# Two graph layers on one core: an earlier read of one bank, the setup work in single pieces, and another order in the last group

## The chip, the core and the metric

The kernel runs on one core of a Trainium2 chip. The metric is the device time of one execution in microseconds (us). The engines are named as in the profile: PE (TensorE, matmuls), PEld (PE's weight loads), DVE (VectorE), ACT (ScalarE), POOL (GpSimd), SP (SyncE, which issues most DMAs here).

## What is computed

The input x is 64 batches of 256 tokens with 512 features, in float32. Cut to what matters, with `h` of the shape of x:

```python
def _layernorm(x, eps=1e-5):
    m, v = mean(x, -1), var(x, -1)
    return (x - m) / sqrt(v + eps)

# layer 0
h = maximum(_layernorm(x), 0)
y = einsum('nm,bmd->bnd', adj, h)
x = x + einsum('bnd,do->bno', y, weight) + bias
# layer 1
h = maximum(_layernorm(x), 0)
q, k, v = h @ Wq + bq, h @ Wk + bk, h @ Wv + bv          # 8 heads of 64
scores = einsum('bqhd,bkhd->bhqk', q, k) / sqrt(64)
scores = scores + (1 - adj) * -1e9
attn = softmax(scores)
x = x + (attn applied to v) @ Wo + bo
```

## The kernel before

**Tiles and groups.** A group is two batches (GB = 2), so there are 32 groups (NG). All of layer 0 runs first, group by group; it leaves each group's residual and its normalized hidden state in DRAM. Then layer 1 runs, group by group.

**Projections.** Each 512x512 projection of a group is done by `project` (L441) in the manner of Strassen and Winograd, on blocks of 256: seven products instead of eight. A product (`product`, L433) is eight matmuls of 128x128 on 256 columns. Three sums of weight blocks (s1, s2, s4, and s3 in place of a block) come from `weight_sums` (L400), once per weight, in four operations (L409 or L411); four sums of data blocks (t1 to t4) come from `Halves.sums` (L427, L431), once per group and projection. The products go into four PSUM banks, called a, b, c and d. The order is: A11·B11 into a, read as u1; A12·B21 into b, finished with u1; S2·T2 added into a, read as u2; S1·T1 into c; S3·T3 added into a, read as u3; then c is finished with u3, and a is released; A22·T4 into d, finished with u3; S4·B22 added into c, finished with u2. In q and k a read makes a partial u on ACT with the bias (L629, two operations of 128x256), and a finish is DVE's add (L485) of a bank and a partial. In v a read is one ACT copy (L646). In layer 0 (prefix w) and in the output projection (prefix o) no partial is made: read and finish both add the bank on DVE straight into a quarter of the residual x, which `RESIDUAL` (L488) names. There a "read" with index 4 adds bank a once more. Partials come from the pool tag "u", which has three buffers.

**Layer 0.** `layer0` (L519): 32 matmuls multiply the adjacency with the group's h (L531, tiles py), ACT copies the result to yT (L541), POOL makes t1 to t4 (tile t_y, L431), and `project` follows. DVE takes statistics of the finished quarters (L582, L587), and ACT makes the next hidden state. The normalization of the input of group g + 2 (`ready`, L491: DVE statistics L42, POOL scales L53 and L54, ACT L506, POOL's bias add L510) is placed between these steps.

**Layer 1.** Per group: `attend` (L713: sums of exponents with `pden` L720, weighted values `pav` L727, reciprocals on DVE L737, division L744, then the sums t_o of the output projection), `score` (L675: products sc L686, scaled and masked on DVE L691, less a bound `top` per query on POOL L697 or, for half of the last group, on DVE L701), exponents on ACT (L704) and sums over keys on POOL (L711, tiles as). Score and attend work on half of the heads at a time (qd 0 and 1). Around them stand `queries_keys` (L617) and `values` (L638) of the next group and `post` (L654), the output projection of the group before. L810 adds the output bias to the residual on POOL.

**What sets the order.** The schedule is by hand. Each engine runs its instructions in the order in which the program issues them. `after(delay, ...)` (L259) puts a piece of work on a list, and `tick()` (L263) issues what is due; `run` (L751) steps a generator, with one tick for each step, so a layer-0 group is eleven ticks: four of the adjacency product and seven of `project`. PSUM banks come from a first-in first-out list (L246, L252). Setup work is hung on layer-0 groups by the list `side` (L757 to L764): the loads of the layer-1 weights, their sums on POOL (for q, k, v, o in groups 4, 6, 8, 10, in ticks 6 to 9), the product of v's bias with Wo (`out_bias`, tile pbo, L387, group 9), and the mask and the bound top from the adjacency (`masks`, L333, groups 12 to 14). In the end, a small product (pf, L833) and a copy (flag, L834) of a test on the statistics of the softmax sums (bad, worst, L828, L829) stand within the last group's output projection, in which S1·T1 comes second. The test decides if a general path is run; in all of these runs it isn't.

Of the kernel before, what the change touches and what calls it, by code (L numbers as in the profile page):

```python
# [198 lines left out]
def kernel(  # L199
# [52 lines left out]
    def give(t):  # L252
        free_banks.append(bank_of.pop(id(t))[0])
# [80 lines left out]
    def masks():  # L334
        adj_sb = tmp.tile([P, NT, N], F32, tag="u", name="adj_sb")
        nc.sync.dma_start(adj_sb, adj.rearrange("(t p) m -> p t m", p=P))
        yield
        pm = bank([P, NT, N], "pm")
        for k in range(NT):
            for t in range(NT):  # L340
                nc.tensor.transpose(pm[:, k, t * P:(t + 1) * P], adj_sb[:, t, k * P:(k + 1) * P], ident)
        nc.vector.tensor_scalar(maskT, pm, -1.0, 1.0, op0=ALU.mult, op1=ALU.add)
        give(pm)
        nc.vector.tensor_scalar(maskT, maskT, MASKED, None, op0=ALU.mult)
        nc.vector.tensor_scalar(adj_sb, adj_sb, -1.0, 1.0, op0=ALU.mult, op1=ALU.add)
        nc.vector.tensor_scalar(adj_sb, adj_sb, MASKED, None, op0=ALU.mult)
        rowmax = small.tile([P, NT], F32, tag="rowmax", name="rowmax", bufs=1)
        nc.vector.tensor_reduce(rowmax, adj_sb, AX.X, ALU.max)
        spread = tmp.tile([P, NT, P], F32, tag="u", name="spread")
        nc.vector.tensor_copy(spread, rowmax[:, :, None].to_broadcast([P, NT, P]))  # L350
        yield
        pt = bank([P, N], "pt")
        for t in range(NT):
            nc.tensor.transpose(pt[:, t * P:(t + 1) * P], spread[:, t, :], ident)
        nc.vector.tensor_copy(top, pt)
        give(pt)
# [23 lines left out]
    def out_bias():  # L380

        wo_sb, bo_r, bv_c = L1["o"]
        bvb = tmp.tile([P, DC, P], F32, tag="u", name="bvb")
        nc.vector.tensor_copy(bvb, bv_c[:, :, None].to_broadcast([P, DC, P]))
        ps = bank([P, D], "pbo")
        for d in range(DC):
            nc.tensor.matmul(ps, bvb[:, d, :], wo_sb[:, d, :], start=(d == 0), stop=(d == DC - 1))  # L387
        nc.vector.tensor_tensor(bo_r, ps, bo_r, op=ALU.add)
        give(ps)
# [7 lines left out]

    W = {}

    def weight_sums(eng, w, n, spread=False):  # L400

        def part(i, j):
            return w[:, 2 * j:2 * j + 2, i * HF:(i + 1) * HF]
        s = {m: const.tile([P, 2, HF], F32, name=f"w{n}_{m}") for m in ("s1", "s2", "s4")}
        ops = ((s["s1"], part(1, 0), part(1, 1), ALU.add), (s["s2"], s["s1"], part(0, 0), ALU.subtract),
               (part(1, 0), part(0, 0), part(1, 0), ALU.subtract), (s["s4"], part(0, 1), s["s2"], ALU.subtract))
        for i, (o, p, q, op) in enumerate(ops):
            if spread:
                after(6 + i, lambda o, p, q, op: eng.tensor_tensor(o, p, q, op=op), o, p, q, op)  # L409
            else:  # L410
                eng.tensor_tensor(o, p, q, op=op)  # L411
        W[n] = dict(s, a11=part(0, 0), a12=part(0, 1), a22=part(1, 1), s3=part(1, 0))

    class Halves:
# [25 lines left out]

    def project(s, halves, by_token, name, read, finish, first_half_first=False):  # L441

        def new(n):
            return bank([P, 2, N], f"{name}{n}")
        pa = new("a")
        product(pa, s, "a11", halves, "b11", by_token, stop=False)
        u1 = read(pa, 1)
        yield
        if first_half_first:
            pc = new("c")  # L450
            product(pc, s, "s1", halves, "t1", by_token, stop=False)
            yield
        pb = new("b")
        product(pb, s, "a12", halves, "b21", by_token)
        finish(pb, u1, 0, 0)
        give(pb)
        yield
        product(pa, s, "s2", halves, "t2", by_token, start=False, stop=False)
        u2 = read(pa, 2)
        yield  # L460
        if not first_half_first:
            pc = new("c")
            product(pc, s, "s1", halves, "t1", by_token, stop=False)
            yield
        product(pa, s, "s3", halves, "t3", by_token, start=False)
        u3 = read(pa, 3)
        finish(pc, u3, 1, 1)
        read(pa, 4)
        give(pa)
        yield  # L470
        pd = new("d")
        product(pd, s, "a22", halves, "t4", by_token)
        finish(pd, u3, 1, 0)
        give(pd)
        yield
        product(pc, s, "s4", halves, "b22", by_token, start=False)
        finish(pc, u2, 0, 1)
        give(pc)
        yield
# [5 lines left out]
        nc.vector.tensor_tensor(o, ps, u, op=ALU.add)  # L485


    RESIDUAL = {1: (0, 0), 2: (0, 1), 3: (1, 1), 4: (1, 0)}  # L488


    def ready(g, moments_at, scales_at, relus_at, biases_at, batches=1):  # L491
# [125 lines left out]
    def queries_keys(g):  # L617

        for n, store in (("q", Q), ("k", K)):
            store[g] = {}  # L620
            bias = L1[n][1]

            def read(ps, m):
                if m == 4:
                    return
                u = partial(f"{n}_{g}", m)
                for c in range(2):
                    f = 2 * (m == 3) + c
                    nc.scalar.activation(u[:, c, :], ps[:, c, :], AF.Identity, bias=bias[:, f:f + 1])  # L629
                return u  # L630

            def finish(ps, u, i, k):
                o = store[g][i, k] = act.tile([P, 2, N], F32, tag=f"{n}{i}{k}", name=f"{n}_{g}_{i}{k}")
                add(o, ps, u)

            yield from project(W[n], HH[g], False, f"{n}_{g}", read, finish)

    def values(g):  # L638
        v = act.tile([P, HQ, GB, NT, HF], F32, tag="yT0", name=f"v_{g}")
        V[g] = {(i, k): v[:, i, k] for i in range(HQ) for k in range(GB)}  # L640

        def read(ps, m):
            if m == 4:
                return
            u = partial(f"v_{g}", m)
            nc.scalar.copy(u, ps)  # L646
            return u

        def finish(ps, u, i, k):
            add(V[g][i, k], ps, u)  # L650

        yield from project(W["v"], HH.pop(g), True, f"v_{g}", read, finish)

    def post(g):  # L654

        xt = X.pop(g)
        halves = HO.pop(g)
        done = []

        def read(ps, n):  # L660
            o = quarter(xt, *RESIDUAL[n])
            add(o, ps, o)

        def finish(ps, u, i, k):
            o = quarter(xt, i, k)
            add(o, ps, o)
            done.append(k)
            if done.count(k) == 2:
                nc.sync.dma_start(out[g * GB + k].rearrange("(t p) d -> p t d", p=P), xt[:, k * NT:(k + 1) * NT, :])

        yield from project(W["o"], halves, True, f"o_{g}", read, finish, first_half_first=g == NG - 1)
# [3 lines left out]
    def score(g, qd, sum_delay):  # L675


        tail = []
        pair = [act.tile([P, GB, 2 * NT, N], F32, tag="h", name=f"a_{g}_{qd}_{c}", bufs=2) for c in range(2)]
        for c in range(2):  # L680
            for b in range(GB):
# [8 lines left out]
                for j in range(2):  # L690
                    nc.vector.scalar_tensor_tensor(a[:, j * NT:(j + 1) * NT, :].rearrange("p k n -> p (k n)"),  # L691
                                                   ps[j], SCALE, maskT_f, op0=ALU.mult, op1=ALU.add)
                    give(ps[j])
                if g == NG - 1 and c == 1:
                    tail.append(a)
                else:
                    nc.gpsimd.tensor_tensor(a, a, top_b, op=ALU.subtract)  # L697
                after(3 + 2 * c + b, exponent, a)
                after(sum_delay + 2 * c + b, key_sum, g, qd, c, b)
        for a in tail:  # L700
            nc.vector.tensor_tensor(a, a, top_b, op=ALU.subtract)  # L701

    def exponent(a):
        nc.scalar.activation(a, a, AF.Exp)  # L704
# [8 lines left out]
    def attend(g, qd):  # L713
# [28 lines left out]
        def divide():  # L742
            for f in range(2):
                nc.vector.tensor_tensor(OT[g][:, 2 * qd + f, :], po[f], rden, op=ALU.mult)  # L744
                give(po[f])
            nc.scalar.activation(den, rden, AF.Identity, accum_out=stats[:, 1, i:i + 1])  # L746
            HO[g].sums(nc.gpsimd if g < NG - 1 else nc.vector, ("t1",) if qd == 0 else ("t2", "t3", "t4"))

        after(1 if g < NG - 1 or qd else 8, divide)

# [4 lines left out]


    side = [[] for _ in range(NG)]  # L757
    mask_steps = masks()
    for i, n in enumerate("qkvo"):
        side[2 + 2 * i].append((load_layer1, n))  # L760
        side[4 + 2 * i].append((lambda n: weight_sums(nc.gpsimd, L1[n][0], n, spread=True), n))
    side[9].append((out_bias,))
    for i in range(3):
        side[12 + i].append((lambda: next(mask_steps, None),))  # L764

    ready(0, (0, 0, 2, 2), (0, 2), (1, 1, 3, 3), (5, 5, 6, 6), batches=2)
    load(1)
    tick()
    turn_adjacency()
    tick()  # L770
    weight_sums(nc.vector, w0_sb, "0")
    load(2)
    tick()
    tick()
# [27 lines left out]
    for g in range(NG):  # L802
# [13 lines left out]
        if g + 1 < NG:  # L816
# [3 lines left out]
            if g + 2 < NG:  # L820
                hidden_sums(g + 2, 2, 3, 4, 5)
                run(post(g))
    while later:
        tick()

    bad = tmp.tile([P, 2 * NG * HQ], F32, tag="u", name="bad")
    worst = small.tile([P, 1], F32, tag="worst", name="worst", bufs=1)
    nc.vector.tensor_scalar(bad, stats.rearrange("p s i -> p (s i)"), BOUND, None, op0=ALU.is_gt)  # L828
    nc.vector.tensor_reduce(worst, bad, AX.X, ALU.max)  # L829
    last = post(NG - 1)  # L830
    run(last, 4)
    pf = bank([1, 1], "pf")
    nc.tensor.matmul(pf, worst, ones[:, 0:1], start=True, stop=True)  # L833
    nc.vector.tensor_copy(flag, pf)  # L834
# [36 lines left out]
```

## Time and profile before

| what | value |
|---|---|
| three runs | 2760.43, 2757.74, 2760.40 us, median 2760.4 |
| the profiled execution's own time | 2759.62 us |
| its span | 2757.9 us |
| granted PE clock, mean | 0.997 |
| PE busy | 2719.9 us, 99% of the span |
| POOL, DVE, ACT busy | 1817.7, 1554.9, 803.6 us |
| 32 layer-0 adjacency products, each | 6.91 us on the chain |
| layer-1 group | 65.40 us from one to the next |
| clock at 0.50 | 194.03 to 200.86, 702.62 to 706.03, 2723.31 to 2726.72 us |

The page's first part gives the busy time of each engine over the whole span. The waits give, for PE, what released it after it had been idle. The chain follows the work that ended last back to the start: a row is a start, a duration and what ran then, or "issue" where the profile shows nothing that was waited for. The timeline gives each instruction's start and duration; in brackets stands how long its engine had been idle before, and who released it. A busy time counts the whole time of an instruction in flight, so neighbouring products overlap by some 0.16 us in the timeline, and the chain's durations are those that add up.

### The profile page before, as it was taken

The numbers are of one execution on the slowest core, as the hardware profiler recorded it, in microseconds if no ns is written. First come the engines' busy times: TensorE is split into PE (matmuls) and PEld (weight loads), VectorE is DVE, ScalarE is ACT, GpSimd is POOL, SyncE is SP. The second block draws the span as 40 slices with busy tenths as digits, with TensorE's granted clock in tenths as the row PEclk, the third lists the DMA queues.
The fourth block names the chain that finished last, engine by engine and source line by source line (L and its number), as shares of the span: only waits on it lengthen the run. The fifth ranks groups of instructions, "written<-read, shape, count | busy, mean of one in ns | idle before, by whom it ended". The sixth has DMA issues, their size and how long they took to land.

```text
span 2757.9 us, 43345 instructions
## 1 busy us (share of the span) xinstructions
PE 2719.9 (99%) x17172; PEld 2242.2 (81%) x17172; DVE 1554.9 (56%) x2783; ACT 803.6 (29%) x1377; POOL 1817.7 (66%) x1424
## 2 busy tenths in 40 slices
PE   8989999999999999999999999999999999999997
PEld 7878888888788888888888888888888888888886
DVE  7877877775455444444555444445555544444456
ACT  3333344342222222222222222222222222222221
POOL 6777676674666666666666666666666666666664
PEclk9999999999999999999999999999999999999999
DMA  7666666663122111111111111111222211111110
GB/s 180 181 170 160 163 170 160 170 160 93 36 61 56 47 47 47 47 46 47 47 47 46 47 47 46 47 47 47 62 62 58 51 47 47 47 46 47 47 47 32
DMA packets 280478, 210.50 MB, mean 76 GB/s; under 512 B 145872, under 2 KB 211920, under 8 KB 280272
## 3 DMA queue, kind: packets, MB, share of 16 engines
q1 hardware_dynamic: 279808, 207.15, 29.0%
q8 instruction: 138, 2.26, 0.3%
q10 hardware_dynamic: 464, 0.52, 0.1%
q14 instruction: 68, 0.56, 0.1%
HBM read 106.96 MB, written 100.66 MB: 75 GB/s over the span
## 4 chain that ended last, share of the span: by engine, by line
PE 95%; DVE 2%; POOL 1%; DMA 1%; issue 1%; ACT 0%; SPq 0%; ACTq 0%; DVEq 0%; POOLq 0%
PE sc L686 8%; PE pav L727 8%; PE py L531 7%; PE pden L720 2%; DVE x L485 1%; DVE a L691 0%; POOL a L697 0%; DMA w_sb<-in_L_gnn_weight_dram 0%; DVE st L582 0%; PE pbo L387 0%; PE o_31a L438 0%; ACT h L561 0%; PE w_1a L438 0%; PE q_29a L438 0%; PE q_27a L438 0%
## 5 line engine op out<-in xcount | busy, mean ns | idle before, releaser
L697 POOL TENSOR_TENSOR a<-a,top 128x1024 f32<-128x1024 f32 x252 | 587.2, 2361 | 711.1 <-DVE a L691 711.1
L691 DVE SCALAR_TENSOR_TENSOR a<-sc,maskT 128x512 f32<-128x512 f32 x512 | 311.9, 680 | 26.8 <-PE sc L686 26.8
L711 POOL TENSOR_TENSOR as<-a 128x512 f32<-128x512 f32 x256 | 319.5, 1288 | 0.0
L704 ACT ACTIVATE a<-a 128x1024 f32<-128x1024 f32 x256 | 264.0, 1057 | 21.5 <-POOL a L697 20.3
L737 DVE RECIPROCAL den<-den 128x128 f32<-128x128 f32 x256 | 216.8, 909 | 71.5 <-ACT den L734 71.4
L686 PE MATMUL sc<-q,k 64*128 64x256 f32 x2048 | 238.4, 383 | 0.0
L727 PE MATMUL pav<-a,v 128*32 128x256 f32 x4096 | 233.2, 379 | 0.0
L686 PEld LDWEIGHTS sc<-q,k 64*128 64x128 f32 x2048 | 194.2, 187 | 44.7 <-issue 26.3
L531 PE MATMUL py<-adjT,h 128*128 128x256 f32 x1024 | 228.7, 382 | 0.9 <-DVE adjT L325 0.9
L531 PEld LDWEIGHTS py<-adjT,h 128*128 128x128 f32 x1024 | 196.1, 192 | 28.5 <-ACT h L506 1.2
L734 ACT ACTIVATE den<-pden 128x512 f32<-128x512 f32 x64 | 38.2, 597 | 594.5 <-issue 459.9
L727 PEld LDWEIGHTS pav<-a,v 128*32 128x32 f32 x4096 | 133.4, 110 | 87.7
L561 ACT ACTIVATE h<-x,nb,rs 128x512 f32<-128x512 f32 x128 | 97.2, 806 | 351.8 <-POOL nb L54 351.7
L510 POOL TENSOR_TENSOR x<-x,b_r 128x512 f32<-128x512 f32 x128 | 160.4, 1284 | 1.0 <-ACT h L506 0.9
L810 POOL TENSOR_TENSOR x<-x,bo_r 128x512 f32<-128x512 f32 x128 | 158.5, 1279 | 0.0
L53 POOL TENSOR_TENSOR rs<-rs,mhalf 128x2 f32<-128x2 f32 (+1 forms) x97 | 78.0, 804 | 117.3 <-DVE nb L52 117.3
L431 POOL TENSOR_TENSOR t_y<-yT,t_y 128x256 f32<-128x256 f32 (+1 forms) x96 | 87.3, 910 | 56.5 <-ACT yT L541 53.9
L746 ACT ACTIVATE den<-den 128x512 f32<-128x512 f32 x64 | 40.4, 632 | 221.4 <-DVE den L737 221.4
L582 DVE BATCH_NORM_STATS2 st<-x 128x6 f32<-128x256 f32 x256 | 96.4, 418 | 4.4
L506 ACT ACTIVATE h<-x,nb,rs 128x512 f32<-128x512 f32 x128 | 93.9, 806 | 10.3 <-POOL nb L54 10.3
L431 POOL TENSOR_TENSOR t_y<-yT 128x256 f32<-128x256 f32 (+1 forms) x96 | 88.0, 917 | 12.3 <-ACT yT L541 9.3
L42 DVE BATCH_NORM_STATS2 st<-x 128x6 f32<-128x512 f32 x128 | 84.9, 663 | 6.5 <-DMA x<-in_x_dram 6.5
(2952 smaller groups left out, 5499.8 us busy)
## 6 DMA issues: line engine op xcount, KB each, us to landing
x<-in_x_dram SPq DMA_DIRECT2D x256, 128.0 KB, 3.5
residual<-x SPq DMA_DIRECT2D x256, 128.0 KB, 2.3
hidden<-r SPq DMA_DIRECT2D x128, 256.0 KB, 4.7
h1T<-hidden SPq DMA_DIRECT2D x64, 512.0 KB, 9.7
x<-residual SPq DMA_DIRECT2D x32, 1024.0 KB, 6.7
out_dram<-x SPq DMA_DIRECT2D x64, 512.0 KB, 3.3
w_sb<-in_L_gnn_weight_dram SPq DMA_DIRECT2D x1, 1024.0 KB, 9.1
wq_sb<-in_L_gnn_Wq_dram SPq DMA_DIRECT2D x1, 1024.0 KB, 8.1
```

Of the source, the lines that this page charges most:

```text
L431: eng.tensor_tensor(self.t[n][:, c, :], self.operand(p, c), self.operand(q, c), op=ALU.subtract)
L510: nc.gpsimd.tensor_tensor(xt[:, t, :], xt[:, t, :], b0_r, op=ALU.add)
L531: nc.tensor.matmul(pss[d][:, b * N:(b + 1) * N], h[:, b * NT + k, d * P:(d + 1) * P], adjT[:, k, :], start=(k == 0), stop=(k == NT - 1))
L561: nc.scalar.activation(h1[:, k * NT + t, :], xt[:, k * NT + t, :], AF.Relu, bias=nb[:, t:t + 1], scale=rs[:, t:t + 1])
L686: nc.tensor.matmul(ps[j][:, kt * N:(kt + 1) * N], k[j * HD:(j + 1) * HD, c, kt * P:(kt + 1) * P], q[j * HD:(j + 1) * HD, c, :], start=True ...
L691: nc.vector.scalar_tensor_tensor(a[:, j * NT:(j + 1) * NT, :].rearrange("p k n -> p (k n)"), ps[j], SCALE, maskT_f, op0=ALU.mult, op1=ALU.add)
L697: nc.gpsimd.tensor_tensor(a, a, top_b, op=ALU.subtract)
L704: nc.scalar.activation(a, a, AF.Exp)
L711: nc.gpsimd.tensor_tensor(AS[c, b], a4[:, :, 0, :], a4[:, :, 1, :], op=ALU.add)
L727: nc.tensor.matmul(po[f][h * 32:(h + 1) * 32, b * N:(b + 1) * N], v[:, k, h * HD + f * 32:h * HD + f * 32 + 32], A[h // 2, b][:, (h % 2) * ...
L737: nc.vector.reciprocal(rden[:, c * P:(c + 1) * P], den[:, c * P:(c + 1) * P])
L810: after(9 + t, lambda t, xt: nc.gpsimd.tensor_tensor(xt[:, t, :], xt[:, t, :], L1["o"][1], op=ALU.add), t, X[g])
```

## The change

**Projection.** S1·T1's bank c is read right behind the product, as c22, with index 0 (in q, k and v a fourth partial on ACT with the bias of the second half of the features; in w and o an add into quarter (1,1) of the residual). After S3·T3 bank a is read as u3, and then added to c22: `finish(pa, c22, 1, 1)` instead of `finish(pc, u3, 1, 1)`. The read with index 4 is gone. `RESIDUAL` is renumbered for it.

**Setup work.** The sums of the weights for q, k, v and o start at groups 4, 8, 12 and 16, one piece in each group, at its second tick. The copy bvb comes in group 13 and the product pbo in group 14. The masks come in seven steps in groups 20 to 26. The sums of w0 are two at once and two in ticks 6 and 7.

**The last group.** Only one of the four subtractions of a score is DVE's, two ticks later; the sums t2 to t4 of group 30 come nine ticks later on POOL, those of group 31 in two parts on DVE; only one tick is run ahead of the last output projection instead of all that are left, so that the bias adds to its residual are issued between its steps; bad and worst come after its fourth step, and the output goes out in quarters of 256 KB.

```diff
@@ -341,9 +341,13 @@
                 nc.tensor.transpose(pm[:, k, t * P:(t + 1) * P], adj_sb[:, t, k * P:(k + 1) * P], ident)
         nc.vector.tensor_scalar(maskT, pm, -1.0, 1.0, op0=ALU.mult, op1=ALU.add)
         give(pm)
+        yield
         nc.vector.tensor_scalar(maskT, maskT, MASKED, None, op0=ALU.mult)
+        yield
         nc.vector.tensor_scalar(adj_sb, adj_sb, -1.0, 1.0, op0=ALU.mult, op1=ALU.add)
+        yield
         nc.vector.tensor_scalar(adj_sb, adj_sb, MASKED, None, op0=ALU.mult)
+        yield
         rowmax = small.tile([P, NT], F32, tag="rowmax", name="rowmax", bufs=1)
         nc.vector.tensor_reduce(rowmax, adj_sb, AX.X, ALU.max)
         spread = tmp.tile([P, NT, P], F32, tag="u", name="spread")
@@ -382,6 +386,7 @@
         wo_sb, bo_r, bv_c = L1["o"]
         bvb = tmp.tile([P, DC, P], F32, tag="u", name="bvb")
         nc.vector.tensor_copy(bvb, bv_c[:, :, None].to_broadcast([P, DC, P]))
+        yield
         ps = bank([P, D], "pbo")
         for d in range(DC):
             nc.tensor.matmul(ps, bvb[:, d, :], wo_sb[:, d, :], start=(d == 0), stop=(d == DC - 1))
@@ -397,7 +402,7 @@
 
     W = {}
 
-    def weight_sums(eng, w, n, spread=False):
+    def weight_sums(eng, w, n, spread=None):
 
         def part(i, j):
             return w[:, 2 * j:2 * j + 2, i * HF:(i + 1) * HF]
@@ -405,10 +410,11 @@
         ops = ((s["s1"], part(1, 0), part(1, 1), ALU.add), (s["s2"], s["s1"], part(0, 0), ALU.subtract),
                (part(1, 0), part(0, 0), part(1, 0), ALU.subtract), (s["s4"], part(0, 1), s["s2"], ALU.subtract))
         for i, (o, p, q, op) in enumerate(ops):
-            if spread:
-                after(6 + i, lambda o, p, q, op: eng.tensor_tensor(o, p, q, op=op), o, p, q, op)
+            todo = lambda o=o, p=p, q=q, op=op: eng.tensor_tensor(o, p, q, op=op)
+            if spread is None:
+                todo()
             else:
-                eng.tensor_tensor(o, p, q, op=op)
+                after(spread[i], todo)
         W[n] = dict(s, a11=part(0, 0), a12=part(0, 1), a22=part(1, 1), s3=part(1, 0))
 
     class Halves:
@@ -440,6 +446,7 @@
 
     def project(s, halves, by_token, name, read, finish, first_half_first=False):
 
+
         def new(n):
             return bank([P, 2, N], f"{name}{n}")
         pa = new("a")
@@ -449,6 +456,7 @@
         if first_half_first:
             pc = new("c")
             product(pc, s, "s1", halves, "t1", by_token, stop=False)
+            c22 = read(pc, 0)
             yield
         pb = new("b")
         product(pb, s, "a12", halves, "b21", by_token)
@@ -461,11 +469,11 @@
         if not first_half_first:
             pc = new("c")
             product(pc, s, "s1", halves, "t1", by_token, stop=False)
+            c22 = read(pc, 0)
             yield
         product(pa, s, "s3", halves, "t3", by_token, start=False)
         u3 = read(pa, 3)
-        finish(pc, u3, 1, 1)
-        read(pa, 4)
+        finish(pa, c22, 1, 1)
         give(pa)
         yield
         pd = new("d")
@@ -485,7 +493,7 @@
         nc.vector.tensor_tensor(o, ps, u, op=ALU.add)
 
 
-    RESIDUAL = {1: (0, 0), 2: (0, 1), 3: (1, 1), 4: (1, 0)}
+    RESIDUAL = {0: (1, 1), 1: (0, 0), 2: (0, 1), 3: (1, 0)}
 
 
     def ready(g, moments_at, scales_at, relus_at, biases_at, batches=1):
@@ -621,11 +629,9 @@
             bias = L1[n][1]
 
             def read(ps, m):
-                if m == 4:
-                    return
                 u = partial(f"{n}_{g}", m)
                 for c in range(2):
-                    f = 2 * (m == 3) + c
+                    f = 2 * (m in (0, 3)) + c
                     nc.scalar.activation(u[:, c, :], ps[:, c, :], AF.Identity, bias=bias[:, f:f + 1])
                 return u
 
@@ -640,8 +646,6 @@
         V[g] = {(i, k): v[:, i, k] for i in range(HQ) for k in range(GB)}
 
         def read(ps, m):
-            if m == 4:
-                return
             u = partial(f"v_{g}", m)
             nc.scalar.copy(u, ps)
             return u
@@ -650,6 +654,9 @@
             add(V[g][i, k], ps, u)
 
         yield from project(W["v"], HH.pop(g), True, f"v_{g}", read, finish)
+
+    def quarter_of(batch, i):
+        return batch.rearrange("(t p) d -> p t d", p=P)[:, :, i * HF:(i + 1) * HF]
 
     def post(g):
 
@@ -665,7 +672,9 @@
             o = quarter(xt, i, k)
             add(o, ps, o)
             done.append(k)
-            if done.count(k) == 2:
+            if g == NG - 1:
+                nc.sync.dma_start(quarter_of(out[g * GB + k], i), o)
+            elif done.count(k) == 2:
                 nc.sync.dma_start(out[g * GB + k].rearrange("(t p) d -> p t d", p=P), xt[:, k * NT:(k + 1) * NT, :])
 
         yield from project(W["o"], halves, True, f"o_{g}", read, finish, first_half_first=g == NG - 1)
@@ -675,7 +684,6 @@
     def score(g, qd, sum_delay):
 
 
-        tail = []
         pair = [act.tile([P, GB, 2 * NT, N], F32, tag="h", name=f"a_{g}_{qd}_{c}", bufs=2) for c in range(2)]
         for c in range(2):
             for b in range(GB):
@@ -691,14 +699,12 @@
                     nc.vector.scalar_tensor_tensor(a[:, j * NT:(j + 1) * NT, :].rearrange("p k n -> p (k n)"),
                                                    ps[j], SCALE, maskT_f, op0=ALU.mult, op1=ALU.add)
                     give(ps[j])
-                if g == NG - 1 and c == 1:
-                    tail.append(a)
+                if g == NG - 1 and c + b == 2:
+                    after(2, lambda a: nc.vector.tensor_tensor(a, a, top_b, op=ALU.subtract), a)
                 else:
                     nc.gpsimd.tensor_tensor(a, a, top_b, op=ALU.subtract)
                 after(3 + 2 * c + b, exponent, a)
                 after(sum_delay + 2 * c + b, key_sum, g, qd, c, b)
-        for a in tail:
-            nc.vector.tensor_tensor(a, a, top_b, op=ALU.subtract)
 
     def exponent(a):
         nc.scalar.activation(a, a, AF.Exp)
@@ -744,7 +750,13 @@
                 nc.vector.tensor_tensor(OT[g][:, 2 * qd + f, :], po[f], rden, op=ALU.mult)
                 give(po[f])
             nc.scalar.activation(den, rden, AF.Identity, accum_out=stats[:, 1, i:i + 1])
-            HO[g].sums(nc.gpsimd if g < NG - 1 else nc.vector, ("t1",) if qd == 0 else ("t2", "t3", "t4"))
+            if g < NG - 2 or qd == 0:
+                HO[g].sums(nc.gpsimd if g < NG - 1 else nc.vector, ("t1",) if qd == 0 else ("t2", "t3", "t4"))
+            elif g == NG - 2:
+                after(9, HO[g].sums, nc.gpsimd, ("t2", "t3", "t4"))
+            else:
+                HO[g].sums(nc.vector, ("t2",))
+                after(1, HO[g].sums, nc.vector, ("t3", "t4"))
 
         after(1 if g < NG - 1 or qd else 8, divide)
 
@@ -755,20 +767,22 @@
 
 
     side = [[] for _ in range(NG)]
-    mask_steps = masks()
+    mask_steps, bias_steps = masks(), out_bias()
+    STEPS = 11
     for i, n in enumerate("qkvo"):
         side[2 + 2 * i].append((load_layer1, n))
-        side[4 + 2 * i].append((lambda n: weight_sums(nc.gpsimd, L1[n][0], n, spread=True), n))
-    side[9].append((out_bias,))
-    for i in range(3):
-        side[12 + i].append((lambda: next(mask_steps, None),))
+        side[4 + 4 * i].append((lambda n: weight_sums(nc.gpsimd, L1[n][0], n, [2 + STEPS * j for j in range(4)]), n))
+    for i in range(2):
+        side[13 + i].append((lambda: next(bias_steps, None),))
+    for i in range(7):
+        side[20 + i].append((lambda: next(mask_steps, None),))
 
     ready(0, (0, 0, 2, 2), (0, 2), (1, 1, 3, 3), (5, 5, 6, 6), batches=2)
     load(1)
     tick()
     turn_adjacency()
     tick()
-    weight_sums(nc.vector, w0_sb, "0")
+    weight_sums(nc.vector, w0_sb, "0", (0, 0, 6, 7))
     load(2)
     tick()
     tick()
@@ -820,15 +834,14 @@
             if g + 2 < NG:
                 hidden_sums(g + 2, 2, 3, 4, 5)
                 run(post(g))
-    while later:
-        tick()
+    tick()
+    last = post(NG - 1)
+    run(last, 4)
 
     bad = tmp.tile([P, 2 * NG * HQ], F32, tag="u", name="bad")
     worst = small.tile([P, 1], F32, tag="worst", name="worst", bufs=1)
     nc.vector.tensor_scalar(bad, stats.rearrange("p s i -> p (s i)"), BOUND, None, op0=ALU.is_gt)
     nc.vector.tensor_reduce(worst, bad, AX.X, ALU.max)
-    last = post(NG - 1)
-    run(last, 4)
     pf = bank([1, 1], "pf")
     nc.tensor.matmul(pf, worst, ones[:, 0:1], start=True, stop=True)
     nc.vector.tensor_copy(flag, pf)
```

## The prediction

> **What bounds the kernel now.** I read the page first. Part 1:
>
> ```profile
> PE 2719.9 (99%) x17172; PEld 2242.2 (81%) x17172; DVE 1554.9 (56%) x2783; ACT 803.6 (29%) x1377; POOL 1817.7 (66%) x1424
> ```
>
> PE is the bound; no other engine is close. The products themselves don't change, so only PE's waits, its extra latencies and the two ends can move. Hence the waits of PE second (us in total, times, longest):
>
> ```profile
> PE pbo L387 <- issue: 5.8, 1, 5.8
> PE o_30a L438 <- DVE x L485: 3.9, 1, 3.9
> PE q_1a L438 <- POOL t_h L431: 2.4, 1, 2.4
> PE pden L720 <- POOL as L711: 2.3, 2, 1.7
> PE w_7a L438 <- ACT yT L541: 1.4, 2, 1.2
> PE w_5a L438 <- ACT yT L541: 1.2, 1, 1.2
> PE w_11a L438 <- ACT yT L541: 1.2, 1, 1.2
> PE w_0a L438 <- DVE x L485: 0.7, 1, 0.7
> PE w_13a L438 <- DVE x L485: 0.7, 1, 0.7
> ```
>
> Single stalls, all in groups with side work or at the ends. Third the chain (start, us, what), which shows what a stall costs in full, and what repeats:
>
> ```profile
> 171.44 6.91 PE py L531 x32
> ...
> 190.50 5.80 issue
> 196.30 5.93 PE pbo L387 x8
> 202.23 6.91 PE py L531 x32
> ...
> 219.50 1.77 PE w_9c L438 x8
> 221.27 6.91 PE py L531 x32
> ```
>
> A clean layer-0 group takes 221.27 − 202.23 = 19.04.
>
> ```profile
> 2601.66 1.73 PE q_30d L438 x8
> 2603.39 1.92 PE q_30c L438 x8
> 2605.31 1.73 PE k_30a L438 x8
> ```
>
> In every q and k the last product (S4·B22) takes 1.92 where the others take 1.73. Fourth the timeline there (start, us, engine, line, in brackets idle before and releaser):
>
> ```profile
> 2601.70 0.84 ACT L629 ACTIVATE u_q<-q_30a,bq_c 128x256 f32<-128x256 f32 x2 [0.72 <-PE q_30a L438]
> 2602.57 0.69 DVE L485 TENSOR_TENSOR q<-q_30c,u_q 128x512 f32<-128x512 f32 x1 [5.29 <-ACT u_q L629]
> 2603.32 1.59 PEld L438 LDWEIGHTS q_30c<-h1T,wq_s 128*128 128x128 f32 x8 [0.33 <-DVE q L485]
> ```
>
> DVE reads bank c only after ACT has made u3 and ends at 2603.26, when the product before is ending too; PE's weight load for S4 then starts late.
>
> **What the Trainium skill says.** "TensorE: Matmul & The Clock Gate", Part 2, step ①: PE pulls weight loads ahead of running matmuls, while matmuls stay in order. The trace agrees: other loads start 0.2 us before their matmuls, this one with them, and the product is 0.19 longer. Same page, Part 1: an idle window of about 3.4 us halves the clock. The windows view shows 0.50 over 194.10 to 200.80, behind pbo's gap; the 2.4 us gap at q_1a also did it (0.65 mean over 4.9 us), so shorter gaps are not safe. "PSUM — Partial Sum Buffer", bank collisions: two engines may not read one bank together. So ACT's u3 and DVE's new add out of bank a come one behind the other, as the order of instructions has it. "SBUF — State Buffer", two separate sides: a DVE operation with two SBUF inputs and a POOL operation exclude each other. Trace: L701 on DVE takes 1.21 alone, about 2.4 beside POOL.
>
> **S1·T1's early read.** It removes the wait ahead of S4: bank c is now read two products earlier. In q and k 64 × (1.92 − 1.73) = 12.2; in w and o, where the read goes straight into the residual, 64 × about 0.045 (w 1.77, o 1.78) = 2.9; v has 1.73 already: 0. Gain 15.1. Bounds: 0, if the late load has a second cause, to 15.1. Added: ACT makes a fourth partial, 0.84 for q, 0.84 for k, 0.58 for v, 2.3 per group of 65.4 on an engine busy 29%; it fits into S3·T3's slot (1.73), and ACT idled 0.72 ahead of u3. If u3 is pushed, DVE's adds are late, but no product reads them. DVE's count is unchanged (the add of u3 to bank c becomes an add of c22 to bank a, 0.69). The new wait is DVE's, on ACT's u3; queued behind it are the adds of banks d and c, and PE needs neither before the next block. S3·T3 into bank a still waits for u2 alone. Four partials go through three "u" buffers, so k's u1 needs the buffer of q's u2, which DVE's last add frees 0.85 after q ends; ACT then ends u1 0.94 later at the latest, about E + 2.75 (E is the end of q, u1 not before E + 1.9); k's second product into bank a starts at E + 3.45. Slack 0.7: cost nothing.
>
> **Weight sums, masks, bias product.** Before, four POOL pieces of 1.27 stand close together in groups 4, 6, 8, 10 and push the next group's scales, ReLU and yT back. Costs, by the chain:
> - py of group 4 starts at 91.71, of group 8 at 171.44: 79.73 against 4 × 19.04 = 76.16, lost 3.57 (the rows of w_5 and w_7).
> - Group 11: 39.73 for two groups against 38.08, lost 1.65.
> - pbo: 202.23 − 171.44 = 30.79 against 19.04, 11.75 too much. Its eight 512-wide matmuls stay; a 256-wide one takes 1.73 / 8 = 0.216 in a product, so at full clock 8 × 2 × 0.216 = 3.46 (an estimate). Saved 8.3: its bvb copy comes a group earlier, so no gap and no half clock.
> - Group 13, masks on DVE (3.4 us in one piece): 39.68 − 38.08 − 0.66 of transposes that stay = 0.94.
> - Group 0: w0's sums in two parts free DVE for the first reads: 0.8.
>
> Gain 15.3. The cover: one piece per group is issued at the second step of py on POOL, which there idles 1.78 ahead of the second t_y (98.81, waits for ACT's yT): 1.27 fits with 0.5 over. Masks in pieces of up to 1.0 on DVE lie beside 1.1 of idle per group, and the read of bank c now comes where DVE has room. If the POOL cover is gone in all 16 groups, each costs up to the 1.2 that a late yT cost before: 19. Value taken: 0. SP moves nothing here. The q_1a stall (4.2 with its half clock) isn't touched.
>
> **The last group.** Let S be the start of the last score (2710.93 before).
> - The key sums of (31,0) no longer stand behind three t_o on POOL (3.75), so pden's waits go and S comes 3.16 earlier. One subtraction comes to POOL there (2.36) and still leaves the sums in time, by 0.15: thin.
> - o_30's second product waited for DVE's read behind L701 until S + 11.29. Now DVE reads first, but t2 stands on POOL behind three subtractions: 2.66 + 3 × 2.36 + 1.27 = S + 11.0; with the port shared up to S + 12.1. Cost −0.3 to 0.8, taken 0.35; the half clock there stays.
> - Last post: t2 and the first read come ahead of t3, t4, so its 0.74 stall goes. But the four bias adds to x_31 (1.27 each on POOL), which were done before, are now issued among its steps and wait for DVE's first reads; DVE's second read of bank a waits for them, behind it stand bad and worst, behind those PE's pf, and behind pf S3·T3. By steps from the start of post: DVE read at 4.5; POOL 7.1 and 9.6; DVE 10.3; pf 10.9; S3·T3 at 11.1 instead of 9.04. Cost 1.0 (if the adds overlap better) to 2.2, plus 1.7 of half clock, as the gap is nearly 4 us: taken 2.9.
> - Output by quarters on SP, four DMAs of 256 KB for two of 512 KB: the last took 3.7 from issue to landing; 128 KB pieces land in 2.3. Gain 1.0 (0.5 to 1.4).
>
> Net gain 3.16 − 0.35 − 2.9 + 1.0 = 0.9, bounds −1.5 to 4.
>
> **Sum.** 15.1 + 15.3 + 0.9 = 31.3. The profiled execution took 2759.6 (span 2757.9 and 1.7 around it), 0.8 under the median of 2760.4: 2759.6 − 31.3 = 2728.3, so 2728.
>
> **Rivals.**
> - The wait ahead of S4 is replaced by another one (ACT late, or a load that waits for something else released at the same time): 2728 + 15.1 = 2743. For: one product's 0.19 can hide several releasers. Against: v, whose u3 takes 0.58 on ACT instead of 0.84 and so ends 0.26 earlier, has no such delay, and after the change bank c has been read over 2 us before S4.
> - The POOL pieces aren't covered: up to 19 back, 2738 to 2747. For: margin 0.5. Against: the pieces that stalled came four in a row.
> - Slower: the ring of "u" buffers. If exponents (1.06 each) stand ahead of k's u1 on ACT, two make it 2.1 late; less 0.7 of slack, 1.4 × 32 groups = 45: 2728 + 45 = 2773. It decides from 0.7 of lateness, and ends above 2760 from 1.7. Against: at q_30 the last exponent ends at 2603.49, and k's u1 isn't due before 2607.
> - The change doesn't act: the tail's gain is eaten whole and the pieces only move their stalls. That lies within the bounds above.
>
> **How the numbers follow.** Main case 0.70, 2728 with its own range 2723 to 2734 (tail and small terms); S4's wait stays 0.14, 2743; POOL uncovered 0.10, up to 2747; ring of buffers 0.06, 2773. The range 2722 to 2747 holds the first three. A measurement tells 0.2% (5.5 us) from no change: faster needs under 2755. Faster 0.92, same 0.03, slower 0.05.
>
> **What would show it.** In the chain q's and k's last products read 1.73, not 1.92; pbo takes 3.5 with no issue row ahead; PE's waits on yT in w_5, w_7, w_11 and on pden are gone; a wait of 3 to 4 us stands at o_31a's third product or pf, released by DVE. I am wrong if q_c stays at 1.92, if waits on "u", yT or t_y come up in many groups, or if the span doesn't fall by some 15 us in each layer.

## The result, and the profile after

The changed kernel took 2728.1 us (median of 4 runs, 2727.19 to 2729.09) against 2759.9 (4 runs, 2757.74 to 2760.43): ratio 0.9886, 95% interval 0.9869 to 0.9903, so 31.8 us less. The profiled executions took 2759.62 and 2727.19 us, 32.4 apart.

The page's first part of the changed kernel, to be held against the one shown of before:

```profile
PE 2699.5 (99%) x17172; PEld 2252.1 (83%) x17172; DVE 1539.6 (56%) x2781; ACT 874.2 (32%) x1537; POOL 1823.1 (67%) x1426
```

PE has as many instructions as before and is still the bound. (The trace shows each matmul of the program as two, so the eight of a product are four in the code, and the 32 of py sixteen.) ACT has 160 more: the fourth partials. The waits of PE in the changed kernel:

```profile
...
PE o_30a L444 <- POOL t_o L437: 4.5, 1, 4.5
PE pf L846 <- DVE worst L844: 3.2, 1, 3.2
PE q_1a L444 <- POOL t_h L437: 2.4, 1, 2.4
...
PE w_0a L444 <- DVE x L493: 0.3, 1, 0.3
```

All waits on yT, on pden's sums and ahead of pbo are gone. The one at o_30a has a new releaser, POOL's t2 in place of DVE's read, and one at pf is new. The chain at q_30, where S4·B22 is the second row:

```profile
2572.37 1.73 PE q_30d L444 x8
2574.09 1.73 PE q_30c L444 x8
```

1.73 instead of 1.92. The chain at pbo, now in group 14:

```profile
279.01 1.73 PE w_13c L444 x8
280.74 3.43 PE pbo L392 x8
284.17 6.91 PE py L539 x32
```

No "issue" row ahead of it, and 3.43 instead of 5.93. By stages, from the starts of the same products in the two traces (us, minus is earlier than before; the three parts alone are e1 to e3 below):

| stretch | whole change | early read alone | setup alone | last group alone |
|---|---|---|---|---|
| start to q_0 | -16.7 | -4.2 | -14.5 | -0.7 |
| q_0 to v_31 | -13.4 | -13.5 | -0.6 | 0.0 |
| v_31 to the end | -2.4 | +0.3 | +1.5 | -2.3 |
| span | -32.5 | -17.4 | -13.7 | -3.0 |

Within layer 1 each group is 0.44 shorter: 0.20 in q, 0.19 in k, 0.05 in o. The first stretch also holds the start, in which w_0's first product begins between 0.9 us earlier and 0.2 later than before in these traces.

### The profile page after: what moved, and what is told of

Read it like the earlier page. It is cut to its first block, busy times and chain, and to the rows that moved or that the text cites. A ratio compares the mean times of both kernels' runs of the same rounds, so it can differ in the third digit from the quotient of the medians.

```text
span 2725.3 us, 43511 instructions
## 1 busy us (share of the span) xinstructions
PE 2699.5 (99%) x17172; PEld 2252.1 (83%) x17172; DVE 1539.6 (56%) x2781; ACT 874.2 (32%) x1537; POOL 1823.1 (67%) x1426
## 4 chain that ended last, share of the span: by engine, by line
PE 98%; POOL 1%; DVE 1%; DMA 0%; issue 0%; ACT 0%; DVEq 0%; ACTq 0%; POOLq 0%
PE sc L694 8%; PE py L539 8%; PE pav L733 8%; PE pden L726 2%; POOL a L705 1%; PE v_31a L444 0%; PE q_31a L444 0%; PE q_27a L444 0%; PE v_22a L444 0%; PE v_18a L444 0%; PE q_18a L444 0%; PE q_14a L444 0%; PE v_9a L444 0%; PE v_5a L444 0%; PE q_5a L444 0%; PE v_30a L444 0%
## 5 line engine op out<-in xcount | busy, mean ns | idle before, releaser
L705 POOL TENSOR_TENSOR a<-a,top 128x1024 f32<-128x1024 f32 x254 | 593.7, 2373 | 699.1 <-DVE a L699 699.1
L710 ACT ACTIVATE a<-a 128x1024 f32<-128x1024 f32 x256 | 270.8, 1058 | 22.4 <-POOL a L705 22.4
```

## Experiments: the three parts alone

**e1, the early read alone.** The kernel before with this edit, the renumbered `RESIDUAL` and the fourth partials:

```diff
             product(pc, s, "s1", halves, "t1", by_token, stop=False)
+            c22 = read(pc, 0)
             yield
...
-        finish(pc, u3, 1, 1)
-        read(pa, 4)
+        finish(pa, c22, 1, 1)
```

> The kernel before with the early read of S1*T1 and the add of u3's bank alone. My theory (S4 of q and k starts late because bank c is read just ahead of it): q's and k's last products 1.73 instead of 1.92, 64 x 0.19 + 64 x 0.045 = 15.1 us less, about 2745, ratio 0.9945. Rival (another release takes the wait's place): the last products stay at 1.92 and the time within 3 us of 2760. Rival (ring of three partials): waits of PE at k's products, over 2760.

Measured 2741.7 us, ratio 0.9932 (0.9919 to 0.9946): 18.0 less, about 3 more than expected. The stages say where: layer 1 gives 13.5, layer 0 gives 4.2 where 1.4 was counted. What is more lies in groups with side work: the waits of w_5, w_7 and w_11, on a late yT, are 0.7, 1.2 and 0.7 us instead of 1.2, 1.4 (two) and 1.2, that of w_13, on DVE, is gone, and pbo's gap is 5.1 instead of 5.8. (A wait at w_0 grew from 0.7 to 2.1, but w_0 began 0.9 earlier.) The setup work also removes these waits, so this part of the two gains is one and the same.

**e2, the setup work alone.** The kernel before with the spread `weight_sums`, the steps of masks and bias product, and the new `side` list:

```diff
-        side[4 + 2 * i].append((lambda n: weight_sums(nc.gpsimd, L1[n][0], n, spread=True), n))
-    side[9].append((out_bias,))
-    for i in range(3):
-        side[12 + i].append((lambda: next(mask_steps, None),))
+        side[4 + 4 * i].append((lambda n: weight_sums(nc.gpsimd, L1[n][0], n, [2 + STEPS * j for j in range(4)]), n))
+    for i in range(2):
+        side[13 + i].append((lambda: next(bias_steps, None),))
+    for i in range(7):
+        side[20 + i].append((lambda: next(mask_steps, None),))
```

> The kernel before with the spread weight sums, masks and bias product alone. My theory: the stalls at w_0, w_5, w_7, w_11, w_13 and at pbo go, 15.3 us less, about 2745, with pbo at 3.4 us. Rival (pieces not covered by POOL's idle time): new waits on yT or t_y in up to 16 groups, 1.2 us each, so as little as nothing gained.

Measured 2743.5 us, ratio 0.9940 (0.9926 to 0.9953): 16.1 less. Layer 0 gives 14.5. No wait on yT or t_y is left. In this trace the last stage is 1.5 us longer than before, though nothing was changed there: it has a second stretch at half clock, from 2692.62 to 2696.03, behind pden's two waits (2.3 us together). And the gap of 2.4 us at q_1a has no such stretch behind it here, which makes q_1 1.0 shorter (see the last section).

**e3, the last group alone.** The kernel before with the changed `score`, `divide`, `post` and ending, in short:

```diff
-            HO[g].sums(nc.gpsimd if g < NG - 1 else nc.vector, ("t1",) if qd == 0 else ("t2", "t3", "t4"))
+            elif g == NG - 2:
+                after(9, HO[g].sums, nc.gpsimd, ("t2", "t3", "t4"))
...
-    while later:
-        tick()
+    tick()
+    last = post(NG - 1)
+    run(last, 4)
```

> The kernel before with the last group's order alone. The trace of the changed kernel shows 2.4 us gained between the start of v_31 and the end: 3.16 at pden, minus 0.6 and 0.8 at o_30, minus 1.4 at the last S3*T3, plus about 1.1 at the end and what was shifted. Expected 2 to 3 us less, about 2757; if the last group's gains hung on the early read, less than 1.

The trace shows 3.0 less, 0.7 of them ahead of q_0, where nothing was changed; the medians show nothing: 2759.45 us, ratio 0.9998 (0.9990 to 1.0007). Its 13 runs lie between 2755.5 and 2762.6. So the last group's order gained something in the profiled execution and nothing that the median can tell. The parts named in the expectation come to 1.5, not to 2.4: o_30 costs 0.4 in all, and not 0.6 and 0.8. Together the three parts alone give 18.0 + 16.1 + 0.2 = 34.3 against 31.8 for the whole. In layer 0 of the traces they give 19.5 against 16.7: some 2.8 us of waits that e1 and e2 share.

## Experiments: why S4 was late, and how much room there is

**e4, a shorter u3.** Order of reads as before, one ACT copy per partial in q and k (their bias is left out):

```diff
-                for c in range(2):
-                    f = 2 * (m == 3) + c
-                    nc.scalar.activation(u[:, c, :], ps[:, c, :], AF.Identity, bias=bias[:, f:f + 1])
+                nc.scalar.copy(u, ps)
```

> The kernel before with q's and k's partials made by one ACT copy without the bias (the bias of q and k is left out), as v does it: ACT takes 0.58 instead of 0.84 for u3, so DVE's read of bank c ends about 0.26 us earlier, with the old order of reads. My theory (only the lateness of that read delays S4's weight load): the last products fall from 1.92 to about 1.73, 64 x 0.19 = 12 us less, about 2748. Rival (the delay hangs on which bank is read, or on a second release): 1.92 stays and the time within 3 us of 2760.

Measured 2748.5 us, ratio 0.9957 (0.9943 to 0.9971), 11.1 less than the runs of before beside it. The chain of e4 at q_30:

```profile
2590.78 1.73 PE q_30c L438 x8
```

and its timeline, with ACT's u3, DVE's read of bank c, and the start of S4's weight loads and matmuls:

```profile
2589.09 0.59 ACT L627 COPY u_q<-q_30a 128x512 f32<-128x512 f32 x1 [0.96 <-PE q_30a L438]
2589.71 0.69 DVE L485 TENSOR_TENSOR q<-q_30c,u_q 128x512 f32<-128x512 f32 x1 [5.04 <-ACT u_q L627]
...
2590.46 0.57 PEld L438 LDWEIGHTS q_30c<-h1T,wq_s 128*128 128x128 f32 x3
2590.62 0.60 PE L438 MATMUL q_30c<-h1T,wq_s 128*128 128x256 f32 x2
```

S4's first matmul is due 1.73 behind that of the product before. In e4 the read ends at 2590.40, 0.22 ahead of that time, the load starts 0.06 later, and the matmul is on time. Before, the matmul was due at 2603.23, the read ended 0.04 behind that, at 2603.26, and load and matmul started together at 2603.32: 0.09 late, and the product then took 0.10 more. The 0.19 is gone with the old order of banks, so the lateness of that read is enough to explain it; layer 1 is 12.3 shorter in this trace, and its last stage takes 2.0 back with a second stretch at half clock, as in e2. The other projections of the kernel before lie on the same line: in v the read ends 0.22 ahead of the time due and S4 takes 1.73, in w and o 0.11 ahead and S4 takes 1.77 and 1.78. A quarter of a microsecond decides.

From e5 on the differences are those of the medians from the changed kernel's 2728.1. The runs of before that were taken beside these had medians of 2758.9 (e5 to e8) and 2760.4 (e9 to e12), so reckoned by way of before each would be 1.0 us higher or 0.5 lower.

**e5 and e6, two and four pieces in a tick.** The changed kernel with

```diff
-        side[4 + 4 * i].append((lambda n: weight_sums(nc.gpsimd, L1[n][0], n, [2 + STEPS * j for j in range(4)]), n))
+        side[4 + 4 * i].append((lambda n: weight_sums(nc.gpsimd, L1[n][0], n, [2 + STEPS * (j // 2) for j in range(4)]), n))
```

for e5, and for e6, in place of the same line,

```diff
+        side[4 + 4 * i].append((lambda n: weight_sums(nc.gpsimd, L1[n][0], n, [2] * 4), n))
```

> The changed kernel with two pieces of a weight's sums in each group's second tick, in half as many groups. By my prediction's reckoning the cover was 1.78 us of POOL's idle time for one piece of 1.27; by that two pieces overrun it by 0.8, in 8 groups: 6 us slower. By the trace of the changed kernel 0.73 us of idle time is left behind a piece and the last of the sums that S2*T2 needs ends 1.6 us ahead of need: a second piece then costs nothing, and the time stays within 1 us of 2728.

> The changed kernel with all four pieces of a weight's sums in one tick, in four groups. Three more pieces are 3.8 us, less 0.73 of idle time and 1.6 us of slack: S2*T2 of w about 1.5 us late in four groups, 6 us slower than the changed kernel, about 2734, with waits of w_4a, w_8a, w_12a, w_16a on POOL t_y. If spreading doesn't matter but only the tick, no wait and 2728.

e5 took 2728.7 us, ratio 0.9891 (0.9876 to 0.9906), with the same layer-0 period to 0.01 us; e6 2734.0, ratio 0.9910 (0.9896 to 0.9923), 5.9 over the changed kernel. Each of e6's four groups is 1.28 longer, 5.1 together. The waits of PE in e6 that the changed kernel doesn't have are at w_4a, w_8a, w_12a and w_16a:

```profile
PE w_8a L444 <- POOL t_y L437: 0.8, 1, 0.8
...
PE w_4a L444 <- POOL t_y L437: 0.8, 1, 0.8
```

POOL's timeline of the changed kernel behind a piece says why one or two are free:

```profile
94.47 1.28 POOL L413 TENSOR_TENSOR wq_s<-wq_sb 128x512 f32<-128x512 f32 x1
...
97.17 0.72 POOL L437 TENSOR_TENSOR t_y<-yT,t_y 128x256 f32<-128x256 f32 x1 [0.73 <-ACT yT L549]
97.86 0.73 POOL L437 TENSOR_TENSOR t_y<-yT 128x256 f32<-128x256 f32 x1
98.66 0.72 POOL L437 TENSOR_TENSOR t_y<-yT,t_y 128x256 f32<-128x256 f32 x1
```

0.73 of idle time is left, and the last sum that S2·T2 needs (the last row) ends at 99.38, while S2·T2 starts at 101.00. The room is 0.73 + 1.6, not the 0.5 of the prediction, which looked at POOL's idle time alone and not at who waits for its results.

**e7, four buffers for the partials.** All tiles of the tag "u" with bufs=4; one of the seven places:

```diff
-        return tmp.tile([P, 2, N], F32, tag="u", name=f"u{n}_{name}")
+        return tmp.tile([P, 2, N], F32, tag="u", name=f"u{n}_{name}", bufs=4)
```

> The changed kernel with four u buffers in place of three. My theory (the ring has slack): within 1 us of 2728 and no product shorter. Rival (the ring is near its limit and costs something somewhere): some waits of ACT's partials go and the time falls by a microsecond or more.

Measured 2726.9 us, ratio 0.9886 (0.9871 to 0.9901), the changed kernel's own; from group 1 on every product of the two traces stands within 0.05 us of the other, less a constant. The ring of three costs nothing; with the fourth partial it has the slack that was worked out.

## Experiments: the waits that are left at the ends

The chain of the changed kernel in the last output projection (start, us, what):

```profile
2708.19 0.69 DVE x L493
...
2708.95 4.55 POOL x L824 x3
...
2713.53 0.69 DVE x L493
2714.22 0.14 DVE bad L843
...
2714.39 0.30 DVE worst L844
...
2714.73 0.19 PE pf L846 x2
2714.91 1.92 PE o_31a L444 x8
```

Between these rows stand only "issue" rows of at most 0.07. DVE's first read releases POOL's bias adds, these release DVE's second read of bank a, and bad, worst and pf follow.

**e8, pf later.** `run(last, 6)` in place of `run(last, 4)` ahead of bad, worst and pf:

```diff
-    run(last, 4)
+    run(last, 6)
```

> The changed kernel with bad, worst and pf behind the sixth step of the last output projection instead of the fourth. If pf's place is the cause of the wait of 3.16 us at the last S3*T3, it goes. If the bias adds on POOL are (DVE's read of bank a waits for them), S3*T3 only gains the 0.6 to 0.7 us of bad, worst and pf: about 1 us less, with the wait of some 2.4 us now at o_31a, released by DVE.

Measured 2729.2 us, ratio 0.9895 (0.9880 to 0.9910). Nothing gained. The waits of PE in e8:

```profile
PE o_31a L444 <- DVE x L493: 2.7, 1, 2.7
...
PE pf L846 <- DVE worst L844: 1.2, 1, 1.2
```

The first wait is the one that was expected behind the bias adds (2.4 reckoned), 0.5 shorter than the one at pf in the changed kernel; but bad and worst now stand behind DVE's add of bank d, and PE waits a second time ahead of S4.

**e9, the bias adds earlier.** The four adds to x_31 are issued with the single tick ahead of the projection, bad and worst stay behind step 4, and only pf goes behind step 6:

```diff
-            after(9 + t, lambda t, xt: ...
+            after(9 + t if g < NG - 1 else 8, lambda t, xt: ...
...
     nc.vector.tensor_reduce(worst, bad, AX.X, ALU.max)
+    run(last, 2)
     pf = bank([1, 1], "pf")
```

> The changed kernel with group 31's bias adds on POOL issued ahead of its output projection, and pf behind its sixth step while bad and worst stay behind the fourth. The late read in e8 was released by those adds. If they are the cause of the wait at the last S3*T3, it starts at about 8.0 us from the start of the projection in place of 10.45: 2.5 us less than the changed kernel, about 2725.5, with no wait of PE within o_31. If DVE's own work sets that read, the wait stays over 1.5 us.

Measured 2724.1 us, ratio 0.9871 (0.9855 to 0.9888): 4.0 less than the changed kernel, and no run of the two overlaps; in the trace 2.95, of which 2.4 from v_31 on, where 2.5 was reckoned. What remains of the wait in e9:

```profile
PE o_31a L444 <- DVE x L493: 0.8, 1, 0.8
```

S3·T3 starts at 7.96 us from the projection's start, as reckoned. The bias adds were the cause, and pf came on top. (The bias adds alone, with pf in its old place, were not run.) The 0.8 that is left was not expected: S1·T1 comes second here, so S3·T3 follows straight on S2·T2 and waits for DVE to read the bank, 0.69.

**e10, group 1's sums earlier.**

```diff
-    hidden_sums(1, 1, 2, 8, 9)
+    hidden_sums(1, 1, 2, 7, 7)
```

> The changed kernel with group 1's sums t3 and t4 (t_h) issued two ticks earlier, ahead of a score's four subtractions on POOL. The wait at q_1a (2.4 us) and its half clock (1.9 us) go: 4.3 us less, about 2724. If POOL has no room there, pden's first product waits for as instead.

Measured 2723.8 us, ratio 0.9870 (0.9854 to 0.9886): 4.3 less, again with no overlap of runs; q_1 to k_1 is 4.48 shorter in the trace, the wait and its half clock are gone and nothing took their place. This wait was in the kernel before, and the change did not touch it.

**e11, group 30's sums on DVE.**

```diff
-                after(9, HO[g].sums, nc.gpsimd, ("t2", "t3", "t4"))
+                after(9, HO[g].sums, nc.vector, ("t2", "t3", "t4"))
```

> The changed kernel with group 30's t2 to t4 on DVE, where nothing stands between a read and the subtraction, instead of behind three subtractions on POOL. t2 is then there about 8.1 us from the score's start, not 11.9: the wait of 4.5 us at o_30a falls to about 1 and its half clock goes, up to 5 us less; the sums as of POOL then come near their need, which can take 1 us back. About 2723.5.

The expectation was wrong: 2730.6 us, ratio 0.9890 (0.9874 to 0.9907), 2.5 over the changed kernel, though the lowest of its four runs lies among that kernel's. The wait ahead of S2·T2 did fall from 4.5 to 0.6, and S2·T2 started 3.96 earlier. But the timeline of e11 on DVE and PE goes on:

```profile
2684.71 1.27 DVE L437 TENSOR_TENSOR t_o<-oT,t_o 128x512 f32<-128x512 f32 x1
2685.90 2.84 DVE L437 TENSOR_TENSOR t_o<-oT 128x512 f32<-128x512 f32 x1
2688.66 1.75 DVE L437 TENSOR_TENSOR t_o<-oT,t_o 128x512 f32<-128x512 f32 x1
2690.34 2.28 DVE L703 TENSOR_TENSOR a<-a,top 128x1024 f32<-128x1024 f32 x1
...
2693.87 3.78 PE L444 MATMUL o_30a<-wo_sb,t_o 128*128 128x256 f32 x8 [4.12 <-DVE x L493]
```

Beside POOL's subtractions and key sums the three DVE sums take 1.27, 2.84 and 1.75 us where DVE alone took 0.68 to 0.69 for such a sum (group 31's in e9). Behind them and L703 stands DVE's read of bank a, and S3·T3 waits 4.1 us for it. The stall moved one product on: 0.6 and 4.1 us of waits in place of 4.5. That alone is nearly neutral; the loss in the trace is half clock. In this execution the stall brought 6.8 us of it in place of 3.4 (o_30 longer by 1.8), and the gap at pf, which has none in the changed kernel, brought 3.4 (1.6 more).

**e12, all three.** The edits of e9, e10 and e11 in one kernel:

```diff
-                after(9, HO[g].sums, nc.gpsimd, ("t2", "t3", "t4"))
+                after(9, HO[g].sums, nc.vector, ("t2", "t3", "t4"))
...
-    hidden_sums(1, 1, 2, 8, 9)
+    hidden_sums(1, 1, 2, 7, 7)
...
+            after(9 + t if g < NG - 1 else 8, lambda t, xt: ...
...
+    run(last, 2)
     pf = bank([1, 1], "pf")
```

> The three edits of e9, e10 and e11 in one kernel. If they don't meet, 2.5 + 4.3 + 4.5 = 11 us less than the changed kernel, about 2717; if the last group is bound by POOL's sums as after the earlier o_30, 2719 to 2720 with a wait at pden on POOL as.

Measured 2721.3 us, ratio 0.9857 (0.9841 to 0.9874): 6.8 under the changed kernel and the fastest of these runs, though it carries e11's stall. Neither forecast was right on the cause: PE's wait is at o_30a's S3·T3 (4.1 us), as in e11, not at pden. In this trace that stall brought 3.4 us of half clock, not 6.8, and o_30 is only 0.6 longer than in the changed kernel. e9 and e10 without e11 was not run; by their own gains (4.0 and 4.3) it would come to about 2720, an estimate.

## Why the prediction was right, step by step

- **S4's wait.** 12.2 for q and k and 1.4 for o were reckoned in layer 1, 13.4 came; 1.4 in w. e4 shows the cause by itself. The traces agree with "TensorE: Matmul & The Clock Gate", Part 2, step ① of the Trainium skill, on which the step rested: S4's first load starts 0.21 us ahead of its matmul in the changed kernel, 0.16 ahead in e4, and with the matmul in the kernel before.
- **Setup work.** 15.3 reckoned, with w's 1.4 together 16.7 in layer 0; 16.7 came. pbo lost its gap and its half clock and takes 3.43 (3.46 reckoned; in the trace of before the copy bvb on DVE starts at 195.8, takes 0.43, and pbo starts at 196.30, so the copy was what it waited for), groups 4 to 8 gave 3.8 (3.57 and four times 0.045), group 11 gave 1.7. What the sum did not say is that the two parts aren't independent: alone, the early read would have taken some 2.8 of it.
- **The cover.** Right in its result, wrong in its measure: 0.5 us of room was feared, over 2 us are there (e5, e6). The rival "POOL uncovered" was therefore given too much weight.
- **The last group.** 0.9 reckoned, 2.4 in the profiled execution, about nothing in e3's median; the prediction's bounds were -1.5 to 4. Its terms: S came 3.16 earlier, as reckoned to the hundredth. o_30's S2·T2 came 0.6 later from S and its end 0.4 later (0.35 taken). The mis-sized term is the last S3·T3: 11.1 us from the start of post reckoned, 10.45 measured, since the fourth bias add came behind DVE's second read of bank a and not ahead of it; and no half clock came in this execution, where 1.7 was counted. So 1.4 was lost there, not 2.9. The end gave 1.1 (1.0 taken): 3.16 - 0.4 - 1.4 + 1.1 makes the 2.4. The wait of 3.2 us at pf, released by DVE, is the one that was forecast.
- **The rivals.** No wait took the place of S4's (e1: nothing on k's products), and the ring of "u" buffers had its slack (e7), as the trace of before had said.

The sum was 31.3, the profiled executions lie 32.4 apart, the medians 31.8. For the two layers this is the mechanism, stage by stage; that the whole comes within about 1 us is in part luck, since one stretch at half clock in the last group is worth 1.7.

## What to carry to other kernels

A bank should be read as soon as its product is done, and the reader that closes a chain should be the one whose bank nobody waits for: a read that ended 0.22 us ahead of the time at which the next matmul into its bank was due cost nothing here, one that ended 0.04 us behind it cost 0.19, 64 times. How much side work an engine can take is told by the slack of those who wait for its results, more than by its own idle time. When work is moved to a faster engine to end one stall, everything that stands behind it there has to be reckoned too: in e11 the stall only moved on by one product, and there DVE's sums took up to four times as long beside POOL.

## What the runs showed that was not expected

The same gap doesn't always cost the same clock. Ahead of pf PE idles 3.16 us in the changed kernel and in e5 alike. PE's timeline of the changed kernel, the product behind the gap:

```profile
2714.73 0.19 PE L846 MATMUL pf<-ones,worst 128*1 128x1 f32 x2 [3.16 <-DVE worst L844]
2714.84 1.99 PE L444 MATMUL o_31a<-wo_sb,t_o 128*128 128x256 f32 x8
```

and of e5:

```profile
2713.88 0.19 PE L846 MATMUL pf<-ones,worst 128*1 128x1 f32 x2 [3.16 <-DVE worst L844]
2714.00 3.78 PE L444 MATMUL o_31a<-wo_sb,t_o 128*128 128x256 f32 x8
```

1.99 against 3.78, and the product after it is slow in e5 too. The windows view gives a clock of 1.00 over that stretch in the changed kernel and 0.75 in e5. The halved stretches in all these traces last 3.41 us or twice that (6.83), but for the last one, which the end cuts off, and within a trace their starts lie whole multiples of 3.41 apart (2689.31 - 685.69 = 2003.62 = 587 x 3.413 in the changed kernel): a window that runs by itself, as "TensorE: Matmul & The Clock Gate", Part 1, of the Trainium skill has it. So it seems to be the place of a gap in that window that decides: behind the same gap of 3.2 us at pf lie no time at half clock (the changed kernel), 3.41 us (e11) or 6.83 us (e5), which costs nothing, 1.6 or 3.0 us; the gap of 2.4 us at q_1a brings 3.41 us in the changed kernel and none in e2, e5 and e6. A tail with several such gaps then scatters by some us between runs, which is probably why e3's runs lie 7 us apart. It fits that the mean granted clock is 0.997 in its six runs up to 2758.9 us and 0.996 in its seven from 2759.5 on, but only one of the 13 was traced.
